# Cross-attention in float32 products: the values as seven block products, turned by way of DRAM and by block turns, and w_t x kept in DRAM

## The chip, the cores and the metric

The kernel runs on one core of one Trainium2 chip. The metric is the device time of one execution in microseconds; several runs are taken and the median is shown. A profile of one execution by the hardware profiler says which engine did what when. The engines are PE (matrix products; PEld are its weight loads), DVE (VectorE), ACT (ScalarE), POOL (GpSimd) and SP (SyncE, which here only issues transfers). Each works through a list of its own, in order, and waits on semaphores for the others.

## What is computed

The reference, cut to what matters, for B = 32 batches of x and y (`ctx_2048`) with C = 256 channels and N = 1024 places, all in float32:

```python
x_q = jnp.einsum('oc,bcn->bno', w_qk, y)
x_k = jnp.einsum('oc,bcn->bon', w_qk, x)
x_v = jnp.einsum('oc,bcn->bon', w_v, x) + b_v[None, :, None]
energy = jnp.einsum('bnc,bcm->bnm', x_q, x_k)
attention = jax.nn.softmax(energy, axis=-1)
attention = attention / (1e-07 + attention.sum(axis=1, keepdims=True))
x_r = jnp.einsum('bcn,bnm->bcm', x_v, attention)
x_r = jax.nn.relu(jnp.einsum('oc,bcn->bon', w_t, x - x_r) + b_t[None, :, None])
return x + x_r
```

## The kernel before

**The algebra.** The weights are multiplied with each other once at the start. Keys of a batch are k = -(w_qk^T w_qk) x, so that energy is -(y^T k). The values are multiplied by w_t beforehand: u = -(w_t w_v) x. What the output needs of x beside them is w_t x + b_t. So a batch needs k, u and w_t x from x, the energy from y and k, the softmax, and the sum of u over the attention.

**Exactness.** Every operand of a product is held as two float32r tiles, a high part (rounded, a copy on ACT) and a low part (what is left, a subtraction on POOL or DVE). A product is then three matmuls: high by high, high by low, low by high (`ORDER`).

**Seven products.** Keys, w_t x and energies are products of matrices cut in 2 x 2 blocks, done with seven block products instead of eight (the sums and differences of blocks that this takes are `x_sum`, `y_sum`, `key_sum` on the operands, and `key_block`, `x_block`, `energy_add`, `energy_block` on the results). A block product is 128 x 128 weights by 512 columns, so a batch takes 21 matmuls for k, 21 for w_t x and 4 x 21 for the energies. The values u are not done in this way before the change: they are needed with the place n on the partitions (as weights of the attention products), and `values` gets them so by taking pieces of x as weights and `vws` (w_t w_v, 256 columns) as what streams: 48 matmuls of 256 columns. ACT then takes the high parts from PSUM (`value_high`) and DVE the low parts (`value_low`), 128 x 1024 each, twice a batch.

**A batch.** Eight tiles of 128 rows of the energy, in four pairs `E0` to `E3` of seven products each. Each pair ends in blocks that DVE adds up while it takes the row's least (`energy_block`, a custom instruction and one that reads its accumulator). ACT takes the exponential, DVE the reciprocal of the sum, ACT the high part (`h`) and DVE the low part (`l`) of the shares, and DVE (for the first tile ACT) adds the shares up for the division by columns (`sum`, in `acc`). Products `A` (tile, half of channels c, half of columns h; three matmuls each, 96 a batch) add up u by the shares in PSUM banks 4 to 7. When all eight tiles are in, `cols`, `inv` and `turn` on DVE make the columns' inverse sums, `div` on DVE multiplies, `join` on POOL adds w_t x from the tile `xe`, `pos` on ACT is the relu, `add` is a transfer issued by POOL that adds x from DRAM, and `st` stores.

**PSUM.** Of eight banks, 0 to 3 hold energies and keys, 4 to 7 the attention; between `div` of one batch and the first `A` of the next, banks 4 to 7 serve the values and w_t x.

**The order** is written out by hand as three lists of words (`FIRST`, `STEADY` for each batch, `LAST`), where a + or - ahead of a word moves it one batch on or back. A word is a small function: `E0P1` is the first product of pair 0, `xP3` the third product of w_t x, `V01` half of the values. `InOrder` keeps the lists' order on PE, DVE, ACT and POOL; the transfers on SP have no such chain and stand as the scheduler puts them. Since `InOrder` issues everything, nearly every row of the profile bears its line, L62; instructions are told apart by the names of tiles: `gws`, `tws` the weights of k and w_t x, `xf` and `gf` the forms of x and k, `yd` and `ysum` those of y, `uf` those of u, `efs` those of the shares, `rs` results in passing, `raws` what is loaded, `z` the output.

Of the kernel before, what the change touches and what calls it, by code (L numbers as in the profile page):

```python
# [17 lines left out]
def kernel(  # L18
# [54 lines left out]
    def value(v):  # L73
        return v.bitcast(F32)

    class Ring:


        def __init__(self, name, places, shape, dtype=F32):
            self.tile = mem.tile([P, places, *shape], dtype, name=name)  # L80
            self.places, self.next, self.held = places, 0, {}

        def __getitem__(self, key):
            if key not in self.held:
                self.held[key] = self.tile[:, self.next % self.places]
                self.next += 1
            return self.held[key]
# [5 lines left out]
    RIGHT = {1: 0, 2: 2, 3: 3, 4: 7, 5: 4, 6: 6, 7: 5}  # L93
    T1, T3, T2, T4 = range(4, 8)
# [11 lines left out]
    vws = mem.tile([P, FORMS, KC, C], F32R, name="vws")  # L106
    xf = mem.tile([P, FORMS, 8, MB], F32R, name="xf")
# [6 lines left out]
    xe = mem.tile([P, KC, N], F32, name="xe")  # L114
    rct, rc = acc.rearrange("p (j r) -> p j r", r=G32), acc
    raws = Ring("raws", 2, [N])
    sums = Ring("sums", 4, [2, MB])
    efs = Ring("efs", 4, [FORMS, MH, MB], F32R)
    rs = Ring("rs", 4, [MB])
    small = Ring("small", 60, [1])  # L120
# [36 lines left out]

    gt, tt = (
# [4 lines left out]
    raws.held["y", 0, 0] = xe[:, 0]  # L163
# [4 lines left out]
    def load_y(b, q):  # L168
        load(
            raws["y", b, q].rearrange("p (k n) -> p k n", k=KC),  # L170
            y[b].rearrange("(k p) n -> p k n", p=P)[:, :, ts(q, MB)],
        )
# [71 lines left out]
    once("Sth", act.copy, tt[:, HIGH], wtT)  # L244
    once("Stl", pool.tensor_tensor, tt[:, LOW], wtT, value(tt[:, HIGH]), ALU.subtract)
# [40 lines left out]
    left_blocks("T", tws, lambda: wtT)  # L286

# [6 lines left out]

    def x_high(b, k):
        act.copy(flat(xf[:, HIGH, 2 * k : 2 * k + 2]), raws["x", b, k])

    def x_low(b, k):
        at = slice(2 * k, 2 * k + 2)
        pool.tensor_tensor(  # L300
            flat(xf[:, LOW, at]), raws["x", b, k], flat(value(xf[:, HIGH, at])), ALU.subtract
        )
# [19 lines left out]
    for k in range(KC):  # L322
        word(f"ldx{k}", load_x, k)
        word(f"ldy{k}", load_y, k)
        word(f"xh{k}", x_high, k)
        word(f"xl{k}", x_low, k)
        word(f"xTh{k}", sums_high, ("x13", "x24")[k], xf, slice(4 + 2 * k, 6 + 2 * k))
        word(f"xTl{k}", sums_low, ("x13", "x24")[k], xf, slice(4 + 2 * k, 6 + 2 * k))
# [6 lines left out]
    def products(name, bank, left, right, where, first):  # L335
        for i, w in zip((1, 2, 3, 4, 5, 6, 7), where):
            words[f"{name}P{i}"] = lambda b, i=i, w=w: product(
                banks[:, bank[w]], left(i), right(i), i in first
            )

# [4 lines left out]
        "k", KB, lambda i: lambda j: gws[:, j, LEFT[i]], lambda i: lambda m: xf[:, m, RIGHT[i]],  # L345
# [40 lines left out]
    for tail, name, at in ((0, "kA", KT3), (1, "kB", KT4)):  # L386
# [5 lines left out]
    XB = dict(a=6, b=4, c=5)  # L392
    products(
        "x", XB, lambda i: lambda j: tws[:, j, LEFT[i]], lambda i: lambda m: xf[:, m, RIGHT[i]],
        "abcacaa", (1, 2, 5),
    )
    xb = {w: banks[:, at] for w, at in XB.items()}

    def x_read(b, j):
        act.activation(rs["x", b, j], xb["a"], AF.Identity, bias=xbias[:, j // 3])  # L400

    def x_block(b, j, w, c, h):
        dve.tensor_tensor(xe[:, c, ts(h, MB)], xb[w], rs["x", b, j], ALU.add)

    for j in range(1, 4):
        word(f"xr{j}", x_read, j)
    word("xc11", x_block, 1, "b", 0, 0)
    word("xc22", x_block, 3, "c", 1, 1)
    word("xc12", x_block, 2, "c", 0, 1)
    word("xw21", lambda b: act.activation(xe[:, 1, :MB], xb["a"], AF.Identity, bias=xbias[:, 1]))  # L410

    VP = (2, 3)

# [475 lines left out]
```

## Time and profile before

| | |
|---|---|
| time, median of 3 runs (lowest to highest) | 1828.92 us (1828.8 to 1829.51) |
| span of the profiled execution | 1827.7 us, 1.2 us under the median |
| HBM read, written | 101.58 MB, 33.55 MB, 74 GB/s over the span |
| instructions | 25492, of them 8680 matmuls and as many weight loads |
| transfers | 66 loads of x and 64 of y on SP, 62 adding loads of x on POOL, 66 stores |
| PE in 40 equal slices of the span | 9 tenths or more in all, 8 in the last |

Busy times in the profile are unions of the instructions' times; a mean in a group is the length of one instruction, in which the start of the next can already lie. Idle time stands with what ended it.

### The profile page before, as it was taken

The numbers are of one execution on the slowest core, as the hardware profiler recorded it, in microseconds if no ns is written. First come the engines' busy times: TensorE is split into PE (matmuls) and PEld (weight loads), VectorE is DVE, ScalarE is ACT, GpSimd is POOL, SyncE is SP. The second block draws the span as 40 slices with busy tenths as digits, with TensorE's granted clock in tenths as the row PEclk, the third lists the DMA queues.
The fourth block names the chain that finished last, engine by engine and source line by source line (L and its number), as shares of the span: only waits on it lengthen the run. The fifth ranks groups of instructions, "written<-read, shape, count | busy, mean of one in ns | idle before, by whom it ended". The sixth has DMA issues, their size and how long they took to land. (4 is left out here: it accounts for less than half of the span.)

```text
span 1827.7 us, 25492 instructions
## 1 busy us (share of the span) xinstructions
PE 1819.0 (100%) x8680; PEld 1518.6 (83%) x8680; DVE 1683.3 (92%) x3200; ACT 1363.2 (75%) x2128; POOL 1365.8 (75%) x975
## 2 busy tenths in 40 slices
PE   9999999999999999999999999999999999999998
PEld 7888888888888888888888888888888888888886
DVE  6999999999999999999999999999999999999998
ACT  7778777777777787777877778777777777787765
POOL 7877777777787777877777777777777787777863
PEclk9999999999999999999999999999999999999999
DMA  2123232232312322223323223232332322323222
GB/s 90 47 81 89 61 81 58 81 93 58 92 52 76 93 62 89 66 62 92 78 74 81 58 81 92 59 82 58 81 93 58 93 51 77 93 62 89 58 81 69
DMA packets 46722, 136.78 MB, mean 75 GB/s; under 512 B 4480, under 2 KB 5376, under 8 KB 46592
## 3 DMA queue, kind: packets, MB, share of 16 engines
q1 hardware_dynamic: 37248, 102.25, 15.7%
q0 software_dynamic: 8928, 32.51, 10.8%
q8 instruction: 68, 1.11, 0.2%
q14 instruction: 62, 0.51, 0.1%
q10 hardware_dynamic: 416, 0.39, 0.1%
HBM read 101.58 MB, written 33.55 MB: 74 GB/s over the span
## 5 line engine op out<-in xcount | busy, mean ns | idle before, releaser
L62 PE MATMUL banks<-efs,uf 128*128 128x512 f32 x3072 | 763.5, 389 | 0.0
L62 PEld LDWEIGHTS banks<-efs,uf 128*128 128x128 f32 x3072 | 576.7, 188 | 120.4
L62 PE MATMUL banks<-gf,ysum 128*128 128x512 f32 x1524 | 411.1, 393 | 0.2
L62 ACT ACTIVATE banks<-banks,small 128x1024 f32<-128x1024 f32 x256 | 278.2, 1087 | 177.0 <-DVE small L62 174.5
L62 DVE SCALAR_TENSOR_TENSOR efs<-banks,small,efs 128x512 fp32r<-128x512 f32 x512 | 367.7, 744 | 4.2 <-ACT efs L62 1.4
L62 ACT ACTIVATE efs<-banks,small 128x512 fp32r<-128x512 f32 x512 | 339.8, 691 | 37.4 <-DVE small L62 15.2
L62 DVE SCALAR_TENSOR_TENSOR acc<-banks,small,acc 128x512 f32<-128x512 f32 x448 | 326.1, 746 | 10.6 <-ACT efs L62 5.6
L62 PEld LDWEIGHTS banks<-gf,ysum 128*128 128x128 f32 x1524 | 279.3, 188 | 66.7 <-POOL gf L62 11.2
L62 POOL TENSOR_TENSOR sums<-raws 128x256 f32<-128x256 f32 (+1 forms) x188 | 189.1, 1013 | 191.6 <-DMA raws<-in_ctx_dram 191.5
L62 PE MATMUL banks<-gf,yd 128*128 128x512 f32 x1158 | 307.3, 391 | 0.5 <-DVE rs L62 0.5
L62 PEld LDWEIGHTS banks<-gf,yd 128*128 128x128 f32 x1158 | 214.6, 188 | 46.2 <-DVE rs L62 1.8
L62 DVE CUSTOM_DVE_ANT_0 banks<-banks,rs,small 128x512 f32<-128x512 f32 x254 | 192.4, 758 | 34.8 <-PE banks L62 12.4
L62 ACT COPY rs<-banks 128x512 f32<-128x512 f32 (+1 forms) x286 | 167.2, 585 | 68.2 <-PE banks L62 67.8
L62 POOL TENSOR_TENSOR xf<-raws,xf 128x1024 fp32r<-128x1024 f32 x62 | 148.8, 2400 | 83.0 <-ACT xf L62 83.0
L62 PEld LDWEIGHTS banks<-vws,xf 128*128 128x128 f32 x1536 | 194.5, 191 | 10.1 <-DVE z L62 4.2
L62 PE MATMUL banks<-vws,xf 128*128 128x256 f32 x1536 | 198.7, 282 | 0.0
L62 POOL TENSOR_TENSOR gf<-sums,gf 128x1024 fp32r<-128x1024 f32 (+1 forms) x95 | 191.6, 2046 | 0.6 <-ACT gf L62 0.6
L62 DVE CUSTOM_DVE_ANT_0 banks<-banks,rs 128x512 f32<-128x512 f32 x254 | 179.8, 708 | 11.8 <-PE banks L62 0.5
L62 POOL TENSOR_TENSOR ysum<-sums,ysum 128x1024 fp32r<-128x1024 f32 x64 | 154.2, 2409 | 48.2 <-ACT ysum L62 48.2
L62 PE MATMUL banks<-xf,tws 128*128 128x512 f32 x651 | 177.3, 389 | 0.0
L62 PE MATMUL banks<-xf,gws 128*128 128x512 f32 x651 | 163.9, 391 | 0.0
L62 POOL TENSOR_TENSOR z<-z,xe 128x1024 f32<-128x1024 f32 x62 | 148.1, 2410 | 13.6 <-DVE z L62 13.6
(105 smaller groups left out, 2357.3 us busy)
## 6 DMA issues: line engine op xcount, KB each, us to landing
raws<-in_x_dram SPq DMA_DIRECT2D x66, 512.0 KB, 4.2
raws<-in_ctx_dram SPq DMA_DIRECT2D x63, 512.0 KB, 3.9
z<-in_x_dram POOLq DMA_DIRECT2D x62, 512.0 KB, 5.4
out_dram<-z SPq DMA_DIRECT2D x62, 512.0 KB, 3.1
out_dram<-z SPq DMA_DIRECT2D x4, 256.0 KB, 2.0
xe<-in_ctx_dram SPq DMA_DIRECT2D x1, 512.0 KB, 6.5
z<-in_L_xattn_w_t_dram ACTq DMA_DIRECT2D x1, 256.0 KB, 4.5
z<-in_L_xattn_w_v_dram SPq DMA_DIRECT2D x1, 256.0 KB, 5.6
```

The source lines that it names most:

```text
L62: self.last = getattr(self.engine, name)(*args, **kwargs)
```

## The change

**Values.** For batches 1 to 31, u is made as w_t x is: seven block products with weights `mws` (the blocks of w_t w_v and their sums), the right sides shared with those of k and w_t x (`products("u", ...)`). They come out with channels on the partitions. ACT reads bank a four times (`u_read`) and DVE adds three times (`u_block`); the four blocks of 128 x 512 lie in `rs` and are stored to a space in DRAM (`ud`). From there SP loads them in four transfers for each half of the tiles, so that 32 x 32 blocks come to lie where they belong (`u_loaded`, tile `turned`), DVE turns each block in place (`u_turned`), ACT takes the high parts (`u_high`) and POOL the low parts (`u_low`). All this is done a batch ahead. Batch 0 keeps `values`. The places of a half of the tiles are dealt out in blocks of 32, so y is loaded with the same deal, in pieces of 512 bytes, and `y_high` and `y_low` of its second half are two instructions each.

**w_t x** is also made a batch ahead. Its blocks lie in the same three places of `rs` as u's and are stored to another space in DRAM (`xd`); `xe` is gone, and `join` is a transfer issued by POOL that adds from there into `z`.

**Places.** Tiles that went round in turn (`Ring`) now have fixed places by name (`Places`). `xf` has seven forms instead of eight.

**All three lists are new.** Of these the diff shows one line each.

```diff
-    class Ring:
+    class Places:
...
-    vws = mem.tile([P, FORMS, KC, C], F32R, name="vws")
-    xf = mem.tile([P, FORMS, 8, MB], F32R, name="xf")
+    mws = mem.tile([P, FORMS, LEFTS, P], F32R, name="mws")
+    xf = mem.tile([P, FORMS, RIGHTS, MB], F32R, name="xf")
...
-    xe = mem.tile([P, KC, N], F32, name="xe")
+    turned = mem.tile([P, NB // NG, HT, G32], F32, name="turned")
...
-    rs = Ring("rs", 4, [MB])
+    rs = Places(
+        "rs",
+        {
+            ("e", 1): 0, ("e", 2): 1, ("e", 3): 2, ("k", 1): 0, ("k", 2): 1, ("k", 3): 2,
+            ("u", 1): 3, ("u", 2): 4, ("u", 3): 5, ("u", 4): 3,
+            ("x", 1): 3, ("x", 2): 4, ("x", 3): 5, ("x", 4): 3,
+            "F": 4, "corner": 0, "product": 1, "g": 5, "m": 3,
+        },
+        [MB],
+    )
...
+        for k in range(KC):
+            load(
+                y_raw(b, q).rearrange("p (k j n) -> p k j n", k=KC, j=NG)[:, k],
+                y[b].rearrange("(k p) (j h n) -> p k j h n", p=P, j=NG, h=MH)[:, k, :, q],
+            )
...
-    def x_block(b, j, w, c, h):
-        dve.tensor_tensor(xe[:, c, ts(h, MB)], xb[w], rs["x", b, j], ALU.add)
+    def x_block(b, j, w):
+        dve.tensor_tensor(rs["x", b, j], xb(b, w), rs["x", b, j], ALU.add)
+
+    def x_kept(b, j, c, h):
+        load(xspace[b % 2, ts(c, P), ts(h, MB)], rs["x", b, j])
...
+    products(
+        "u", ub, lambda i: lambda j: mws[:, j, LEFT[i]], lambda i: lambda m: xf[:, m, RIGHT[i]],
+        "abcacaa", (1, 2, 5),
+    )
+    def u_read(b, j):
+        act.copy(rs["u", b, j], ub(b, "a"))
+
+    def u_block(b, j, w):
+        dve.tensor_tensor(rs["u", b, j], ub(b, w), rs["u", b, j], ALU.add)
+
+    def u_kept(b, j, c, h):
+        load(uspace[b % 2, ts(c, P), ts(h, MB)], rs["u", b, j])
+
+    def u_loaded(b, h):
+        v = uspace[b % 2].rearrange("(a r) (j h t s) -> j r a h t s", r=G32, j=NG, h=MH, s=G32)
+        for j in range(NG):
+            load(turned[ts(j, G32)], v[j][:, :, h])
+
+    def u_turned(b, h):
+        v = turned.rearrange("p a t r -> p (a t r)")
+        dve.transpose(v, v)
...
+    def u_high(b, h):
+        act.copy(u_tiles(HIGH, h), u_from())
+
+    def u_low(b, h):
+        pool.tensor_tensor(u_tiles(LOW, h), u_from(), value(u_tiles(HIGH, h)), ALU.subtract)
...
     def joined(b, c):
-        pool.tensor_tensor(z[:, c], z[:, c], xe[:, c], ALU.add)
+        pool.dma_start(z[:, c], xspace[b % 2, ts(c, P)], accum_op=ALU.add)
...
     STEADY = """
-        E0P1 kTh0 -inv kTh1 kh22 E0r1 -turn kTl0 -A601 -A611 E0P6 yh11 E0P7 kTl1 E0r2 E0r3
+        E0P1 -A700 kTh1 ysh1 kTl1 +xT1 +xT2 E0r1 E0P7 E0P6 -cols E0r2 +xh1 uh0 +xTh0
```

Three places show how this moves the lists. The first is PE in a steady batch, among the energies of pairs E0 and E1 (`gf,ysum` and `gf,yd`). Before (`vws` are the values, `tws` w_t x):

```order
L62 MATMUL banks<-vws,xf 128x256 x12
L62 MATMUL banks<-gf,ysum 128x512 x3
L62 MATMUL banks<-vws,xf 128x256 x24
L62 MATMUL banks<-gf,yd 128x512 x3
L62 MATMUL banks<-vws,xf 128x256 x12
L62 MATMUL banks<-gf,ysum 128x512 x6
L62 MATMUL banks<-xf,tws 128x512 x3
```

and now:

```order
L62 MATMUL banks<-xf,mws 128x512 x6
L62 MATMUL banks<-xf,tws 128x512 x3
L62 MATMUL banks<-gf,yd 128x512 x3
L62 MATMUL banks<-xf,mws 128x512 x3
L62 MATMUL banks<-gf,ysum 128x512 x6
L62 MATMUL banks<-xf,mws 128x512 x6
L62 MATMUL banks<-gf,ysum 128x512 x3
L62 MATMUL banks<-xf,mws 128x512 x3
L62 MATMUL banks<-gf,yd 128x512 x3
L62 MATMUL banks<-xf,mws 128x512 x3
```

The 48 matmuls of the batch's own values are gone, and 21 of the next batch's (`mws`) stand among the energies instead.

The second place is DVE in the same steady batch, before at pair E1, where a low part of the values stands between two reductions of energies (ISA with `rs` is one, with `small` as a third input one that starts from the least of another):

```order
L62 TENSOR_TENSOR rs<-banks,rs 128x512
L62 ISA banks,small<-banks,rs 128x512
L62 ISA small 128x1
L62 TENSOR_TENSOR uf<-banks,uf 128x1024
L62 ISA banks,small<-banks,rs,small 128x512
L62 ISA small 128x1
L62 ISA banks,small<-banks,rs 128x512
L62 ISA small 128x1
L62 ISA banks,small<-banks,rs,small 128x512
L62 ISA small 128x1
```

and now at pair E2:

```order
L62 TENSOR_TENSOR rs<-banks,rs 128x512 x2
L62 ISA banks,small<-banks,rs 128x512
L62 ISA small 128x1
L62 ISA banks,small<-banks,rs 128x512
L62 ISA small 128x1
L62 ISA banks,small<-banks,rs,small 128x512
L62 ISA small 128x1
L62 TENSOR_TENSOR rs<-banks,rs 128x512
L62 ISA banks,small<-banks,rs,small 128x512
L62 ISA small 128x1
L62 RECIPROCAL small<-small 128x1
```

The low parts are gone from DVE, and adds of u and w_t x (`rs<-banks,rs`) and the turns of `turned` have come. E2's first reductions both stand ahead of the two that start from them, where E1's second pair before the change stood with nothing between.

The third place is SP in one steady batch. Before, a batch has six transfers there:

```order
L718 DMA out_dram<-z 128x1024
L166 DMA raws<-in_x_dram 128x1024
L169 DMA raws<-in_ctx_dram 128x2x512
L718 DMA out_dram<-z 128x1024
L169 DMA raws<-in_ctx_dram 128x2x512
L166 DMA raws<-in_x_dram 128x1024
```

and now:

```order
L210 DMA raws<-in_ctx_dram 128x4x128 x4
L486 DMA uspace<-rs 128x512
L491 DMA turned<-uspace 32x8x128 x4
L486 DMA uspace<-rs 128x512 x3
L459 DMA xspace<-rs 128x512 x4
L844 DMA out_dram<-z 128x1024
L200 DMA raws<-in_x_dram 128x1024
L844 DMA out_dram<-z 128x1024
L200 DMA raws<-in_x_dram 128x1024
L491 DMA turned<-uspace 32x8x128 x4
```

Twenty-four transfers stand where six stood: the loads of u's second half (`ul1`) stand between the first and the other three stores of the next batch's u, and those of the first half (`ul0`) at the end.

337 lines of the change are left out of this document (207 added, 130 removed).

## Prediction

> **What bounds the kernel now.** I read the page first, then the stages, then single instructions. The page gives each engine's busy time, its share of the span and its number of instructions:
>
> ```profile
> span 1827.7 us, 25492 instructions
> PE 1819.0 (100%) x8680; PEld 1518.6 (83%) x8680; DVE 1683.3 (92%) x3200; ACT 1363.2 (75%) x2128; POOL 1365.8 (75%) x975
> ```
>
> TensorE is never idle, but ends of matmuls are modelled, so a busy PE may still be a slow one. The timeline of PE inside one steady batch settles that (start, length and count of runs of like matmuls; two pieces of it):
>
> ```profile
> 868.63 1.59 PE L62 MATMUL banks<-vws,xf 128*128 128x256 f32 x12
> 870.05 0.86 PE L62 MATMUL banks<-gf,ysum 128*128 128x512 f32 x3
> 870.76 3.04 PE L62 MATMUL banks<-vws,xf 128*128 128x256 f32 x24
> ...
> 892.78 4.24 PE L62 MATMUL banks<-efs,uf 128*128 128x512 f32 x18
> 896.86 0.84 PE L62 MATMUL banks<-gf,yd 128*128 128x512 f32 x3
> ```
>
> The 18 matmuls of 512 columns from 892.78 give way to the next run at 896.86: 4.08 us, 0.2267 us apiece. The 24 of 256 columns start at 870.76 and take 3.04 us with the drain of the last (1.59 us for 12, so 12 more cost 1.45): 0.121 us apiece. Nothing stands between them, so PE is bound by its own stream, and a matmul that goes is time that goes. The only thing that PE waits for in the steady state is small:
>
> ```profile
> PEld banks L62 <- POOL gf L62: 11.2, 31, 0.5
> ```
>
> That is 0.36 us in each of 31 batches. The view by stages, with a window of about one batch, tells how far away the next bound is (busy time of PE, weight loads, DVE, ACT and POOL in turn), and the block turn that DVE does once a batch gives the period:
>
> ```profile
> 850.60:906.80 56.20, 56.20 (x270) 47.02 (x269) 52.25 (x101) 42.26 (x67) 42.59 (x31) 1.00 0.28 76
> ...
> 920.52 1.25 DVE L62 STREAM_TRANSPOSE acc<-sc 128x1024 f32<-128x1024 f32 x1
> ...
> 976.97 1.25 DVE L62 STREAM_TRANSPOSE acc<-sc 128x1024 f32<-128x1024 f32 x1
> ```
>
> The period is 976.97 - 920.52 = 56.45 us. At 52.25 in 56.20, DVE is busy for 52.5 us of it and has 4.0 us free. ACT and POOL have about 14 us free, the clock is granted in full, and DMA is busy for 0.28. So PE binds, with VectorE 4 us behind it.
>
> **PE.** Batches 1 to 31 lose the 48 value matmuls of 256 columns and get 21 of 512: 48 x 0.121 = 5.81 us against 21 x 0.2267 = 4.76 us. That is 1.05 us a batch; the total count of the rows before (1536 in a stream of which PE is never out) gives no better figure, so I take 1.0 us, and 31.0 us over 31 batches. PE's own period becomes 55.45 us. Batch 0 keeps the old form and gains nothing.
>
> **DVE.** These are the groups (count, then busy us and mean ns, then idle time before them):
>
> ```profile
> L62 DVE TENSOR_TENSOR rs<-banks,rs 128x512 f32<-128x512 f32 x189 | 130.2, 689 | 21.5 <-PE banks L62 16.8 <-ACT rs L62 0.8
> L62 DVE TENSOR_TENSOR uf<-banks,uf 128x1024 fp32r<-128x1024 f32 x64 | 78.2, 1222 | 0.1
> L62 DVE STREAM_TRANSPOSE acc<-sc 128x1024 f32<-128x1024 f32 x32 | 39.8, 1245 | 1.0
> L62 DVE SCALAR_TENSOR_TENSOR z<-banks,ubias,acc 128x1024 f32<-128x1024 f32 x62 | 79.2, 1278 | 0.0
> L62 DVE CAST xf<-raws 128x1024 fp32r<-128x1024 f32 x1 | 0.7, 695 | 4.4 <-DMA raws<-in_x_dram 4.4
> L62 DVE CUSTOM_DVE_ANT_0 banks<-banks,rs,small 128x512 f32<-128x512 f32 x254 | 192.4, 758 | 34.8 <-PE banks L62 12.4
> L62 DVE RECIPROCAL small<-small 128x1 f32<-128x1 f32 x256 | 40.7, 159 | 28.0 <-ACT banks L62 20.3
> ...
> 914.09 1.27 DVE L62 TENSOR_TENSOR banks<-banks,rs 128x512 f32<-128x512 f32 x2
> ...
> 912.93 1.24 DVE L62 TRANSPOSE_TENSOR_REDUCE parts<-acc 128x32 f32<-128x1024 f32 x1
> ```
>
> Means overlap the instruction behind by some 0.08 us: two adds that take 0.69 each are done in 1.27, so an add costs 0.60, and the 1.24 us at 912.93 gives way at 914.09, after 1.16. A batch loses two low parts of values (2 x 1.14 = 2.28), and gains three adds of u (3 x 0.60 = 1.80) and two block turns. No in-place turn of a tile loaded by DMA is in this trace; the nearest row is the turn of the same size and type, 1.245 us or 1.16 behind another, so 2.32 for two; bounds are 1.4 for the two (a cast of that size out of SBUF takes 0.695) and 2.6 (the slowest pass of 128x1024, `z`, takes 1.278). The lower one would make PE the bound (rival 1), the upper adds 0.3 us to the period. The adds of x keep their number and only write `rs` instead of `xe`. DVE's load becomes 52.5 - 2.3 + 1.8 + 2.3 = 54.3 us of 55.45: 1.15 us free instead of 4.0.
>
> How much of the 4.0 us must stay? Where the second reduction of an energy block takes the least of the first as its start, and stands right behind it, DVE stands for 0.15 us. This piece of its timeline shows it:
>
> ```profile
> 867.74 0.69 DVE L62 CUSTOM_DVE_ANT_0 banks<-banks,rs 128x512 f32<-128x512 f32 x1
> 868.34 0.14 DVE L62 DVE_READ_ACCUMULATOR2_ANT small<- 128x1 f32 x1
> 868.63 0.76 DVE L62 CUSTOM_DVE_ANT_0 banks<-banks,rs,small 128x512 f32<-128x512 f32 x1
> ```
>
> 868.34 + 0.14 = 868.48, and the next starts at 868.63. A batch has eight such pairs; in the old order six are neighbours, in the new one four (the change's rows on DVE show E2's, which are drawn apart): 0.6 us. Seven small steps of the inverse that wait for each other (0.03 each), eight reciprocals with some 0.04 behind each, and the chain of key sums (0.2) make 0.7 more. So about 1.3 us must stay where 1.15 is free: DVE would need 55.6 us for a batch and PE 55.45. The rest of today's idle time (16.8 us for PE at the group `rs`, 20.3 for ACT at the reciprocals, a little over 1 us a batch together) can only go if DVE never runs out of ready work; with two engines at their limit I leave 0.1 of it. **Period 55.7 us**, 0.75 less than now, 31 x 0.75 = 23.2 us.
>
> **A rule that speaks against this.** The Trainium skill (Perfetto Trace Analysis, Identifying the Most-Contended Engine) says that for Tensor the busy share of matmuls is no good measure, and that the share of weight loads is to be set against the occupancy of the others. By it the bound is DVE (92%) and not PE (83% for weight loads), and work moved from PE to DVE can only lose. The trace disagrees as far as PE goes: the runs above follow each other at 0.2267 us without a gap. What the rule would give is the slower rival below, 1886 us, so I keep a chance for it.
>
> **ACT, POOL, DMA: cover that is there.** Rows of what is added:
>
> ```profile
> L62 ACT COPY rs<-banks 128x512 f32<-128x512 f32 (+1 forms) x286 | 167.2, 585 | 68.2 <-PE banks L62 67.8
> L62 ACT ACTIVATE efs<-banks,small 128x512 fp32r<-128x512 f32 x512 | 339.8, 691 | 37.4 <-DVE small L62 15.2 <-PE banks L62 14.8 <-issue 0.2
> L62 ACT ACTIVATE banks<-banks,small 128x1024 f32<-128x1024 f32 x256 | 278.2, 1087 | 177.0 <-DVE small L62 174.5
> L62 ACT CAST uf<-banks 128x1024 fp32r<-128x1024 f32 x64 | 64.9, 1016 | 0.0
> L62 POOL TENSOR_TENSOR z<-z,xe 128x1024 f32<-128x1024 f32 x62 | 148.1, 2410 | 13.6 <-DVE z L62 13.6
> L62 POOL DMA_DIRECT2D z<-in_x_dram x62 | 53.4, 867 | 7.4 <-ACT z L62 7.4
> q1 hardware_dynamic: 37248, 102.25, 15.7%
> z<-in_x_dram POOLq DMA_DIRECT2D x62, 512.0 KB, 5.4
> out_dram<-z SPq DMA_DIRECT2D x62, 512.0 KB, 3.1
> out_dram<-z SPq DMA_DIRECT2D x4, 256.0 KB, 2.0
> ```
>
> ACT gets four copies of 0.585 (2.3 us) a batch, the high parts of values stay at about 1.0, and some 0.3 comes and goes with x and y: about 44.5 of 55.7. POOL gives up two adds of 2.41 (`join`) and takes two low parts of values of the same size; two more DMA issues of 0.87 are 1.7 us, and the shorter first half of x gives back 1.1: about 43.5. Both stay free for over 10 us, which covers this; without the cover it would be 2.3 and 0.6 us a batch. DMA gets 4 MB a batch on top of about 4.3 (four stores of u, eight loads of u, four stores of x, two adding loads of x): 0.28 becomes about 0.6, the pieces of 512 B included, still no bound. The round trip of u has room: `ul1` waits for POOL's `uL0`, which stands by E1's products, and `ut1` stands ahead of E3's first product, with some 63 matmuls of PE, 14 us, between E1's end and there; `ul0` has the 45 matmuls from E3's end to that of the key products, 10 us, less the 2.4 of POOL's `uL1`. Four loads that together take a store and a load of today (2.0 to 5.4 us each by the rows) fit. The adding `join` takes 5.4 us where POOL took 2.4, and only `pos`, `add` and `st` of a tile that is written 55 us later stand behind it.
>
> **Head and tail.**
>
> ```profile
> 1800.00:1815.00 15.00, 14.69 (x64) 11.46 (x63) 14.14 (x31) 8.92 (x14) 1.68 (x1) 1.00 0.34 103
> 1815.00:1828.00 13.00, 5.82 (x26) 4.50 (x24) 8.38 (x12) 0.00 (x0) 3.73 (x3) 0.81 0.22 81
> ```
>
> At the end DVE sets the pace (14.14 of 15.00 busy), so matmuls taken out of the last batch may not shorten it: between 0 and 5 us of the gain is lost there, and I take 2. The head does more for batch 1 earlier; what moves there is gone later, and I take 0 (between -2 and +4).
>
> **The sum.** 1827.7 - 23.2 + 2 = 1806.5 us of span. The median of the runs shown, 1828.92, is 1.2 above the span: **1807.7 us**, put as 1808.
>
> **Rivals.**
>
> 1. PE's own pace. The order hides all that DVE must wait for, and the period is 55.45: 1827.7 - 31.0 + 2 + 1.2 = 1800 us (1795 without the loss at the end and with some of PE's 0.36 us waits gone). For it: PE is fully fed today. Against: 54.3 + 1.3 is over 55.45. Chance 0.2.
> 2. The stores hold ACT. u and x share three places of `rs`, so `xr1` can write only when the store of `ur4` (`ud4`) has landed. Between the two ACT has an exponential and a high part, 1.1 + 0.7 us, against 2.0 us to land a 256 KB store, plus its wait in SP's queue behind `ul1`. Behind `xr1` stand high parts and exponentials, for which DVE waits. A wait of 0.5 to 0.8 us that passes to a DVE without slack gives periods of 56.2 to 56.5: 1823 to 1833 us, near no change. ACT's 11 us of free time speak against it. Chance 0.15.
> 3. Slower: DVE becomes the bound with its waits of today. If it goes on standing for 4.0 us a batch, whoever it waits for, the period is 54.3 + 4.0 = 58.3: 1827.7 + 31 x 1.85 + 1.2 = 1886 us. It decides from 2.15 us of idle time a batch on (56.45 - 54.3); I see 1.3 that must stay, and today's rows show about 1 us that ended with PE or ACT. Chance 0.15.
>
> That the change does not remove the matmuls can be left out: the rows of PE's order show 21 where 48 stood.
>
> **Chances.** The forecast (periods 55.55 to 56.1, 1803 to 1820 us) has 0.5. With rival 1 and the better half of rival 2, faster by over 0.2% (under 1825.3, about what a measurement of this kernel can tell from no change) has 0.75; within 0.2% has 0.10; slower 0.15. The range of 1795 to 1832 us takes in the first rival and most of the second and leaves the third out.
>
> **What would show it.** The rows `xf,mws` should come 0.2267 us apart and the period should be 55.5 to 56 us. DVE should be busy for 54 to 54.6 us of it, the two turns at 1.2 to 1.3 us each, and its idle time should be mostly the 0.15 us stops. PE should show its first real waits, for DVE (weight loads held by `banks<-DVE`), some 0.3 us a batch. Wrong would be: turns far from 1.25 us, DVE idle for over 2 us a batch, `turned` or `rs` waited for by DMA for more than a fraction of a microsecond, or a tail longer by over 5 us.

## The result, and the profile after

| | before | after |
|---|---|---|
| time, median of 4 runs (lowest to highest) | 1829.17 us (1828.8 to 1829.51) | 2164.05 us (2161.0 to 2166.32) |
| ratio to before, 95% interval | | 1.183 (1.1814 to 1.1847) |
| span of the profiled execution | 1827.7 us | 2159.0 us |

The change costs 335 us; 1808 was forecast, so the prediction was wrong in sign and far outside its range. The page of after, the line of busy times:

```profile
PE 1937.6 (90%) x7843; PEld 1473.9 (68%) x7843; DVE 1743.4 (81%) x3295; ACT 1440.1 (67%) x2322; POOL 1399.5 (65%) x1108
```

837 matmuls are gone, as they should be, and nobody is busy all the time any more. One period, from one block turn of `acc` to the next (start, length), and the view by stages for just that stretch (length, busy time and count of PE, weight loads, DVE, ACT and POOL, clock, DMA share, GB/s):

```profile
1041.92 1.23 DVE L62 STREAM_TRANSPOSE acc<-sc 128x1024 f32<-128x1024 f32 x1
...
1109.12 1.23 DVE L62 STREAM_TRANSPOSE acc<-sc 128x1024 f32<-128x1024 f32 x1
```

```profile
1041.92:1109.12 67.20, 60.34 (x245) 45.95 (x244) 54.44 (x105) 44.94 (x73) 43.66 (x35) 0.95 0.46 126
```

This batch takes 67.20 us instead of 56.45. The work itself came out as forecast: 245 matmuls at 0.2267 are 55.5 us, and DVE is busy for 54.4. The engines stand and wait.

Where the loss lies, the same view says for longer stretches: from the first exponential of batch 0 to that of batch 1, and from there to that of batch 31. Before:

```profile
24.79:79.42 54.63, 54.41 (x236) 42.74 (x235) 48.52 (x93) 41.07 (x65) 50.41 (x42) 1.00 0.12 39
79.42:1772.59 1693.17, 1692.96 (x8096) 1415.80 (x8095) 1575.32 (x3002) 1273.21 (x1980) 1281.66 (x901) 1.00 0.27 75
```

After:

```profile
25.18:105.48 80.30, 69.69 (x289) 52.85 (x288) 53.58 (x100) 51.32 (x85) 60.33 (x59) 0.96 0.27 85
105.48:2104.87 1999.39, 1801.34 (x7278) 1370.74 (x7277) 1631.95 (x3090) 1341.81 (x2153) 1306.47 (x1017) 0.96 0.47 126
```

Of the 331.3 us between the two spans, 306.2 lie in the 30 batches of the long stretch (66.65 us each instead of 56.44), and 25.7 in the one stretch ahead of them, the head.

For whom the engines wait, says the view of waits (us in total, times, longest):

```profile
PEld banks L62 <- ACT rs L62: 235.2, 158, 6.3
...
PE banks L62 <- ACT rs L62: 170.6, 65, 5.9
DVE efs L62 <- ACT efs L62: 158.8, 120, 4.6
...
ACT rs L62 <- DMA uspace<-rs: 116.7, 31, 4.7
ACT efs L62 <- DVE acc L62: 92.9, 93, 2.0
```

PE waits for ACT to empty a bank into `rs`, ACT waits once a batch for a store of u, and DVE and ACT wait for each other. SP's queue has waits of its own, those of the loads of u (L491) among them:

```profile
SPq L491 <- POOL uf L62: 236.8, 60, 6.1
```

The timelines of SP, POOL, ACT and PE in one period show how PE's wait comes about; I put the rows in the order of the chain:

```profile
1051.56 0.35 SPq L486 DMA_DIRECT2D uspace<-rs  x1
1058.11 1.88 SPq L491 DMA_DIRECT2D turned<-uspace  x4
1060.09 2.45 SPq L486 DMA_DIRECT2D uspace<-rs  x3
```

```profile
1055.69 2.39 POOL L62 TENSOR_TENSOR uf<-turned,uf 128x1024 fp32r<-128x1024 f32 x1
```

```profile
1066.54 0.69 ACT L62 ACTIVATE rs<-banks,xbias 128x512 f32<-128x512 f32 x1 [3.94 <-DMA uspace<-rs]
```

```profile
1060.65 1.52 PE L62 MATMUL banks<-xf,tws 128*128 128x512 f32 x6
1067.28 1.65 PE L62 MATMUL banks<-xf,tws 128*128 128x512 f32 x3 [5.11 <-ACT rs L62]
1068.72 1.48 PE L62 MATMUL banks<-efs,uf 128*128 128x512 f32 x3
1070.00 1.48 PE L62 MATMUL banks<-gf,yd 128*128 128x512 f32 x3
1071.28 1.23 PE L62 MATMUL banks<-gf,ysum 128*128 128x512 f32 x3
1072.34 0.86 PE L62 MATMUL banks<-xf,tws 128*128 128x512 f32 x3
```

`ul1` may overwrite `turned` only when POOL's `uL0` has read it, at 1055.69 + 2.39 = 1058.08. It stands in SP's queue ahead of the other three stores of u, which so leave at 1060.09 and later, behind four loads. They land slowly, too (median us from issue to landing, view of DMA issues):

```profile
uspace<-rs SPq DMA_DIRECT2D x124, 256.0 KB, 5.5
```

`xr1` writes the place of `rs` that one of them reads, so ACT stands for 3.94 us, and PE, with no bank to write into, starts 5.3 us late (six matmuls from 1060.65 end their turn at 1062.01). That is not all: the next nine need 1071.28 - 1067.28 = 4.00 us instead of 2.04, and three more 1.06 instead of 0.68. The stages show why (clock is the number behind POOL's):

```profile
1060.00:1064.00 4.00, 2.17 (x10) 1.47 (x8) 3.15 (x8) 0.85 (x3) 2.66 (x3) 1.00 0.76 148
1064.00:1070.00 6.00, 2.73 (x7) 2.15 (x7) 1.54 (x4) 3.40 (x6) 0.00 (x0) 0.60 0.55 177
1070.00:1080.00 10.00, 10.00 (x41) 8.04 (x40) 7.53 (x16) 7.65 (x13) 2.77 (x5) 0.90 0.34 91
```

While PE stands, the granted clock falls: 0.60 is the mean of the stage, and narrower windows of the same view show 1.00 up to 1065 and 0.50 from 1065.5 to 1072. The three matmuls from 1068.72 come 0.427 us apart instead of 0.2267. So the late store takes 5.3 + 2.3 = 7.6 us of PE in this period.

### The profile page after: what moved, and what is told of

Same layout as the page of the kernel before. It is cut to its first block, busy times and chain, and to the rows that moved or that the text cites. A ratio compares the mean times of both kernels' runs of the same rounds, so it can differ in the third digit from the quotient of the medians.

```text
span 2159.0 us, 25689 instructions
## 1 busy us (share of the span) xinstructions
PE 1937.6 (90%) x7843; PEld 1473.9 (68%) x7843; DVE 1743.4 (81%) x3295; ACT 1440.1 (67%) x2322; POOL 1399.5 (65%) x1108
## 4 chain that ended last, share of the span: by engine, by line
PE 57%; DVE 13%; ACT 11%; DMA 9%; POOL 5%; issue 4%; SPq 1%; ACTq 0%; DVEq 0%; POOLq 0%
PE banks L62 57%; DMA uspace<-rs 8%; ACT efs L62 5%; DVE acc L62 4%; DVE efs L62 3%; ACT banks L62 3%; DVE banks L62 2%; ACT rs L62 2%; POOL sums L62 2%; POOL xf L62 1%; POOL gf L62 1%; DVE rs L62 1%; ACT acc L62 1%; SPq L491 1%; POOL uf L62 1%
## 5 line engine op out<-in xcount | busy, mean ns | idle before, releaser
L62 PE MATMUL banks<-gf,ysum 128*128 128x512 f32 x1524 | 443.9, 411 | 33.5 <-ACT rs L62 18.8
L62 ACT ACTIVATE efs<-banks,small 128x512 fp32r<-128x512 f32 x512 | 338.8, 689 | 123.7 <-DVE acc L62 92.9
L62 PE MATMUL banks<-gf,yd 128*128 128x512 f32 x1158 | 339.6, 411 | 18.4 <-DVE rs L62 8.8
L62 PE MATMUL banks<-xf,tws 128*128 128x512 f32 x651 | 205.0, 435 | 150.4 <-ACT rs L62 150.4
L62 POOL DMA_DIRECT2D z<-in_x_dram x62 | 63.2, 1024 | 421.5 <-ACT z L62 421.5
L62 ACT COPY rs<-banks 128x512 f32<-128x512 f32 (+1 forms) x410 | 237.6, 588 | 115.6 <-PE banks L62 111.0
L62 DVE TENSOR_TENSOR rs<-banks,rs 128x512 f32<-128x512 f32 x375 | 254.4, 685 | 37.9 <-ACT rs L62 28.7
L62 POOL TENSOR_TENSOR yd<-raws,yd 128x256 fp32r<-128x256 f32 x189 | 161.5, 923 | 186.1 <-ACT yd L62 183.3
L62 PEld LDWEIGHTS banks<-xf,tws 128*128 128x128 f32 x651 | 134.0, 212 | 191.8 <-ACT rs L62 164.4
L62 PE MATMUL banks<-xf,mws 128*128 128x512 f32 x651 | 185.7, 401 | 8.3 <-ACT efs L62 0.7
L62 ACT ACTIVATE rs<-banks,xbias 128x512 f32<-128x512 f32 x125 | 86.2, 689 | 142.5 <-DMA uspace<-rs 112.3
```

Of the source, the lines that this page charges most:

```text
L62: self.last = getattr(self.engine, name)(*args, **kwargs)
```

## The experiments

All are timed in three rounds beside the kernel before (1829 us). "New lists" are `FIRST`, `STEADY` and `LAST` of the change.

### SP's order: e1 and e2

The first theory is that chain. e1 lets SP keep the order of the lists, as the other engines do; in them `ul1` stands behind all stores of u:

```diff
-    pe, dve, act, pool = (InOrder(g) for g in (nc.tensor, nc.vector, nc.scalar, nc.gpsimd))
-    load = nc.sync.dma_start
+    pe, dve, act, pool, sp = (
+        InOrder(g) for g in (nc.tensor, nc.vector, nc.scalar, nc.gpsimd, nc.sync)
+    )
+    load = sp.dma_start
```

> The changed kernel with one edit: SP's transfers are chained in the order of the lists too, as PE, DVE, ACT and POOL are. Theory A (SP's order): in the changed kernel the four loads of u's second half stand ahead of three of the stores of u and wait for POOL's low part, so the stores leave late, ACT waits for them before it overwrites their places in rs (116.7 us in all), PE stands for 5 us a batch and then runs at 0.427 us a matmul for a while. With the stores ahead of the loads, ACT's wait for uspace falls below 40 us, the period from 67 us to 55.5 to 60, the time to 1805 to 1950 us. Theory B (the transfers themselves: 8.3 MB a batch where there were 4.3): stores go on landing after 5 us or more, ACT's wait stays over 90 us, time over 2080 us. Theory C (VectorE at 98%): DVE is busy for over 97% of the period and the time is about 1886 us.

e2 changes one thing in SP's queue, the four loads go behind the last four stores of u:

```diff
+    behind = []
+
     def u_kept(b, j, c, h):
-        load(uspace[b % 2, ts(c, P), ts(h, MB)], rs["u", b, j])
+        behind.append(load(uspace[b % 2, ts(c, P), ts(h, MB)], rs["u", b, j]))
...
-            load(turned[ts(j, G32)], v[j][:, :, h])
+            with ExitStack() as behind_all:
+                for d in behind[-4:]:
+                    behind_all.enter_context(tc.issue_after(d.ins))
+                load(turned[ts(j, G32)], v[j][:, :, h])
```

> The changed kernel with one edit: the loads of u wait in SP's list for the four stores of u traced last; nothing else of SP's list moves (stores of u four in a row, then the four loads). Theory A: this one swap is the cause, so most of what the order by lists gives comes here too: ACT's wait for uspace below 40 us, time below 1980 us and within 3% of the order by lists. Theory A' (SP's list as a whole is bad, not this swap): the order by lists gains and this does not, time over 2080 us. Theory B: neither gains, both over 2080 us. Theory C: about 1886 us with DVE busy for over 97% of the period.

e1 took 2027.38 us (ratio 1.108, 1.1063 to 1.1096), e2 2031.76 (1.1106, 1.1088 to 1.1125). Both gained less than was expected, but the swap alone is worth 132 us, the whole order of SP 137. The amount of the transfers is the same as in after, so it was not their amount that made the stores slow: in e2 the stores of u land in 2.1 us instead of 5.5. In e1 ACT's wait is gone and the one between ACT and DVE has grown (92.9 us in after):

```profile
ACT efs L62 <- DVE acc L62: 118.9, 122, 2.0
...
ACT rs L62 <- DMA uspace<-rs: 3.8, 3, 2.7
```

137 us are 4.4 a batch, not 7.6: waits that the stop had covered take the place of the rest. 198 us stay.

### Two engines on one bank: e4, e3, e6

The timelines of ACT and of DVE in e1 show the next pattern (`efs` of ACT are high parts, `acc` of DVE sums, `efs` of DVE low parts):

```profile
1056.09 0.69 ACT L62 ACTIVATE efs<-banks,small 128x512 fp32r<-128x512 f32 x1 [1.74 <-DVE acc L62]
1058.25 0.69 ACT L62 ACTIVATE efs<-banks,small 128x512 fp32r<-128x512 f32 x1 [0.90 <-DVE acc L62]
```

```profile
1055.24 0.75 DVE L62 SCALAR_TENSOR_TENSOR acc<-banks,small,acc 128x512 f32<-128x512 f32 x1
1056.81 0.75 DVE L62 SCALAR_TENSOR_TENSOR efs<-banks,small,efs 128x512 fp32r<-128x512 f32 x1 [0.81 <-ACT efs L62]
1057.47 0.74 DVE L62 SCALAR_TENSOR_TENSOR acc<-banks,small,acc 128x512 f32<-128x512 f32 x1
1058.97 0.75 DVE L62 SCALAR_TENSOR_TENSOR efs<-banks,small,efs 128x512 fp32r<-128x512 f32 x1 [0.76 <-ACT efs L62]
```

DVE adds up a half of a tile, ACT waits and takes its high part, DVE waits and takes the low part. The low part reads the high part (`efs` is among its inputs), so it waits for ACT in any order. But neither the sum nor the high part reads what the other writes: both only read the bank, yet take turns, in the order of the lists. The old lists mostly give DVE the sum of one half (`sum30 l31`) while ACT takes the other; in the new ones tile 3 has `sum31 h31 l31`, all on one half, and tiles 5 and 7 have a sum and a high part of one half beside each other. The Trainium skill (PSUM — Partial Sum Buffer, PSUM bank collisions raise a hardware error) says that reads of ACT and DVE of one bank must not meet and that the compiler orders such pairs; these rows show that order. e4 puts this pattern into the kernel before, by swapping the halves of the sums of tiles 3, 4, 6 and 7 and nothing else:

```diff
-        ri3 xP5 xr2 +ldx1 h31 exp2 xc11 sum30 l31 xP7 sum31 A100 A000 xr3 ri2 h30 xc22
+        ri3 xP5 xr2 +ldx1 h31 exp2 xc11 sum31 l31 xP7 sum30 A100 A000 xr3 ri2 h30 xc22
...
-        sum41 +xl1 A210 A200 sum50 l50 h41 E3r1 l41 +yh01 l40 E3P6 sum40 -st1 +ldy1 E3P7
+        sum40 +xl1 A210 A200 sum50 l50 h41 E3r1 l41 +yh01 l40 E3P6 sum41 -st1 +ldy1 E3P7
...
```

> The kernel before, with one edit to STEADY: for tiles 3, 4, 6 and 7 the words sum..0 and sum..1 change places, so that ACT's high part and DVE's sum stand side by side on the same half of a tile. Theory D: each of the four pairs makes one engine wait for the other for some 0.6 us; DVE has 4 us a batch free and hides part of it: 1840 to 1900 us, with ACT's wait for DVE acc (below 1 us in all before) over 40 us. Against theory D: 1829 us within 0.3%.

It took 1957.77 us (1.0701, 1.0685 to 1.0717): 128 us from the order of four tiles' sums alone, more than was expected. Three waits of e4:

```profile
ACT efs L62 <- DVE acc L62: 63.9, 68, 1.5
DVE acc L62 <- ACT efs L62: 59.6, 116, 1.1
...
PE banks L62 <- DVE acc L62: 29.3, 29, 1.0
```

Before has no row of the first and the third kind, and of the second

```profile
DVE acc L62 <- ACT efs L62: 5.6, 29, 0.2
```

The third is of another kind than the first two: the moved sum of tile 4 (`sum41`) now reads the bank that `E3P7` writes, and PE stands for it once a batch. So the 128 us are not all turns of ACT and DVE, and no run takes the two apart.

The reverse was tried on e1: e3 swaps the halves for tiles 0, 1, 2, 3, 5 and 7. For tiles 1 and 2 a sum then reads a bank that the next product has overwritten, so their sums are not the reference's.

```diff
...
-        E1P3 +uc2 +ur4 exp3 +ud4 +ud2 +ud3 E1c11 ri3 A111 +xP2 E1c12 sum31 h31 +xr1 l31
-        sum30 +xP5 h30 exp2 +xP6 A011 +xr2 l30 E2P1 ri2 h21 +xc1 sum21 E2P7 +xP7 E2r1
+        E1P3 +uc2 +ur4 exp3 +ud4 +ud2 +ud3 E1c11 ri3 A111 +xP2 E1c12 sum30 h31 +xr1 l31
+        sum31 +xP5 h30 exp2 +xP6 A011 +xr2 l30 E2P1 ri2 h21 +xc1 sum20 E2P7 +xP7 E2r1
...
```

> The order-by-lists kernel (2027 us, period 62.35 us) with one edit to STEADY: for tiles 0, 1, 2, 3, 5 and 7 the words sum..0 and sum..1 change places, so that while ACT takes the high part of one half of a tile, DVE adds the shares of the other half, as the lists before the change mostly had it. Theory D (two engines on one bank take turns): in the new lists ACT's high part and DVE's sum stand side by side on the same half, and one waits for the other each time (ACT efs for DVE acc 118.9 us, DVE efs for ACT efs 74.6, DVE acc for ACT efs 44.9). With the halves apart ACT's wait for DVE acc falls below 50 us and the time to 1870 to 1970 us. Theory R (what is left comes from the transfers of u, x and y and the places in rs): within 1% of 2027 us. Theory V (VectorE's load): DVE's idle time just moves to other waits, time within 1% of 2027 us, and leaving out work on DVE helps more.

2024.53 us (1.1068, 1.1051 to 1.1084), within 3 us of e1 and not the 1870 to 1970 expected: ACT's wait for `acc` fell to 51.8 us, but the moved sums of tiles 1 and 2 now wait for the product ahead of them:

```profile
DVE acc L62 <- PE banks L62: 41.7, 29, 1.4
ACT acc L62 <- PE banks L62: 37.0, 29, 1.3
```

e6 swaps only where nothing moves behind a product, tiles 3, 5 and 7.

> The order-by-lists kernel (2027 us) with sum..0 and sum..1 exchanged in STEADY for tiles 3, 5 and 7 alone, where no energy product overwrites the half that is added later. e3 had moved those of tiles 1 and 2 behind products that overwrite their bank, and they waited for PE in turn. Theory D (ACT and DVE take turns on a bank): ACT's wait for DVE acc falls from 118.9 us to below 60, the stop of PE ahead of the second product of w_t x (33.3 us in 1400) goes, time 1950 to 1995 us. Theory R (transfers and places): 2027 us within 0.5%.

1981.35 us (1.0827, 1.0811 to 1.0844): 46 us less than e1. The wait falls to a quarter, and the store's wait, which the turns had covered, is back:

```profile
ACT rs L62 <- DMA uspace<-rs: 37.9, 31, 3.1
...
ACT efs L62 <- DVE acc L62: 29.8, 62, 2.0
```

### VectorE's load and the way through DRAM: e5 and e8

Two rivals. e5 is e3 without the block turns (the values are left unturned), 2.3 us less of DVE in each batch:

> The kernel of e3_lists_halves_apart without DVE's two block turns of u a batch (leaves out the turning of u's 32 x 32 blocks). Takes 2.3 us a batch, 71 us in all, off DVE. Theory V: the time falls by 45 to 75 us against e3_lists_halves_apart. Theories D and R (engines wait for each other in the order of the lists): by less than 25 us.

2003.56 us (1.095, 1.0931 to 1.0968), 21 us less than e3. e8 is e1 without `ud`, `ul`, `ut`, `uh` and `uL`: u is computed and goes nowhere, the attention uses what lies in `uf`.

> The order-by-lists kernel without u's way after its products (leaves out the stores and loads of u, the block turns and the high and low parts of u; later batches use batch 0's values; u's products, reads and adds stay, and so do the lists). Takes 2 MB of transfers, 2.3 us of DVE, 2.1 of ACT and 4.8 of POOL a batch away. Theory R: 1800 to 1880 us. Theory D and the order of the lists: over 1950 us.

1998.76 us (1.0922, 1.0903 to 1.094), 29 us less than e1, and still 169 us slower than before. In e8 the turns and the way of u are both gone, and most of the loss stays. But e5 and e8 stand on e3 and e1, where other waits can cover what such an edit gains (e14 below shows a case), and the way of w_t x through DRAM stays in both. What the turns and the ways through DRAM are worth in the best form, e12, was not run.

### Single waits: e7, e9 to e12, e14

e7 is put on e6, e9 on e7, e10 and e11 each on e9, e12 on e11. e7 moves `sum10`, for which exp0 waited, behind `E1r1`; e9 gives blocks 1, 3 and 4 of w_t x the places 5, 3, 5 of `rs` and stores u's third block right behind its sum; e10 puts tile 1's low part ahead of `div0` and both its sums ahead of `E0c12`.

```diff
-        +xTl0 sum11 l11 E0c12 l10 E1P1 +ur1 +uc1 +uP6 sum10 exp0 xd2 +ldy0 +ud1 ri0 E1r1
+        +xTl0 sum11 l11 E0c12 l10 E1P1 +ur1 +uc1 +uP6 exp0 xd2 +ldy0 +ud1 ri0 E1r1 sum10
```

> e6_halves_apart_three with the word sum10 (on ACT for tile 1) moved behind E0's second exponential and E1's first read, just ahead of the product that overwrites its bank. In the order-by-lists kernel ACT stands for 1.7 us a batch there for DVE's low part of the same half, and the reads of E1 and u behind it hold PE (0.56 and 0.78 us a batch). Theory D: ACT's wait of acc for DVE efs (49.4 us) falls below 15 us and the time by another 25 to 50 us. Theory R: no change within 0.5%.

> The kernel of the run before (1977.6 us), with w_t x's blocks 1, 3 and 4 in other places of rs (5, 3, 5 instead of 3, 5, 3) and the store of u's third block issued right behind its sum, so that xr1 waits for a store issued about 4 us earlier. What is left there: ACT waits 41 us in all for uspace<-rs, and PE stops ahead of tws. Theory that what is left is single waits in the order: ACT's wait for uspace<-rs falls from 41 us to under 8, the stop of PE ahead of tws goes, and with it 0.6 to 1.3 us a batch, so 1937 to 1960 us. Rival, that the waits stand in series and whatever is taken out comes back at the next one: the wait falls just as much, but the time stays within 8 us of 1977.6, and another wait on banks or acc grows by about as much.

> The kernel of the run before this one (e9), with tile 1's words in another order: the low part of its second half ahead of div0 and of the sums, and both of ACT's sums of this tile ahead of DVE's reduction E0c12, so that DVE's low part and ACT's sum work on different halves. Theory of single waits: E1P7 no longer waits for sum10 (about 1.4 to 1.8 us on PE in each batch so far, PEld and PE on ACT acc 53 and 40 us in all), and 0.7 to 1.5 us a batch go: 20 to 47 us under e9. Rival, waits in series: PE's wait on ACT acc goes and PE's wait on DVE efs (l10, now behind E0c12) or on DVE rs takes its place, within 10 us of e9 or slower.

Three misses: 1977.64 us, 1981.22 and 1979.39, all within 4 us of e6. In e7 PE waits at `E1P7` for the sum that ACT no longer waits behind; in e10 that wait becomes one for `div0`, which reads `acc`. In e9 the wait for the store stayed (44.3 us), now at the second block, `xr2`. Its view of DMA issues gave the reason: over the windows of 1028 to 1031 us and 1031 to 1033 us,

```profile
uspace<-rs SPq DMA_DIRECT2D x2, 256.0 KB, 2.0
...
uspace<-rs SPq DMA_DIRECT2D x1, 256.0 KB, 5.0
```

The late one is issued at 1032.0; POOL's timeline has `join1`, the adding transfer of w_t x, right ahead of it:

```profile
1030.83 0.85 POOL L62 DMA_DIRECT2D z<-xspace  x1
1031.44 2.69 POOL L62 TENSOR_TENSOR ysum<-sums,ysum 128x1024 fp32r<-128x1024 f32 x1
```

e11 puts `join1` behind that instruction of POOL:

```diff
-        E1P7 +ur2 -join0 +ys01 +ys02 +ys04 uL0 -join1 sum01 sum00 h01 l01 E1P6 +yh00
+        E1P7 +ur2 -join0 +ys01 +ys02 +ys04 uL0 sum01 sum00 h01 l01 E1P6 +yh00
...
-        sum31 +xP5 h30 exp2 +xP6 A011 +xr2 l30 E2P1 ri2 h21 +xc1 sum21 E2P7 +xP7 E2r1
+        sum31 +xP5 h30 exp2 +xP6 A011 +xr2 -join1 l30 E2P1 ri2 h21 +xc1 sum21 E2P7 +xP7 E2r1
```

> The kernel of e9 (1981.2 us) with join1, the second adding transfer z<-xspace, issued by POOL one instruction later (behind the low part of y's sums, 1033.8 instead of 1030.8 in the period looked at). In e9 the store of u2 that was issued at 1032.0, beside that transfer, took 5.0 us to land, the other three 2.0, and ACT's xr2 waited 0.94 us for it. If transfers that lie beside each other are what makes the store late: it lands in 2.0 to 2.6 us, ACT's wait for uspace<-rs falls from 44 us to under 10, PE's stop ahead of tws (22 us in 1100, about 1.2 us a batch with the slow matmul behind it) goes, and the time falls by 15 to 38 us, to 1943 to 1966. If waits stand in series: ACT's wait falls just as much, and the time stays within 8 us of 1981. If the store's 5 us has another cause: the wait stays at 35 to 45 us.

1939.67 us (1.06, 1.0582 to 1.0617), 41.6 less than e9, a little more than expected. The wait is gone (4.5 us in all instead of 44.3).

e12 then puts `E1P6` ahead of `E1P7`, so that PE has a product that does not need tile 1's bank:

> The kernel of e11 with E1's sixth product ahead of its seventh, as pair E3 has them, so that PE has 0.68 us of work that needs no bank of tile 1 while ACT adds up sum10. Single waits: PE's stop for ACT acc (93 us, 3 us a batch by both kinds) falls by about 0.68 us a batch, 15 to 25 us under e11. Waits in series: PE stops at E1P6 for E1r1 instead (rs), and the time stays within 8 us of e11.

1931.39 us (1.0548, 1.0518 to 1.0577), 8 us less than e11: about half of the least that was expected of a single wait (15 us), since PE now stops for `E1r1` (its timeline shows 0.79 us at that place). With e13 below it is the fastest form with the change, and slower than the kernel before.

e14 puts the edits of e9 and e11 on e1, without those of e6 and e7:

> The kernel of e1 (2027.4 us, SP's queue in the lists' order) with e9's places and store and e11's later join1, and no change in the order of tile 1's, 3's, 5's or 7's words. Between e7 and e11 these were worth 38 us. If transfers and turns on a bank add up: 1980 to 1995 us. If the turns cover the transfers' wait (DVE and ACT stand for each other anyway): 2010 to 2025. If the wait for the store costs more there, since it holds up turns too: under 1975.

2027.29 us (1.109, 1.1071 to 1.1108), nothing gained on e1's 2027.38. So the two costs do not add up: as long as ACT and DVE wait for each other on a bank, they cover the late store, and what the transfers cost shows only when the turns are gone.

### The rest: e13, e15, e16

e13 is e12 with two waits between DVE and ACT taken out, at tiles 1 and 4:

```diff
-        +xTl0 sum11 l11 E0c12 l10 E1P1 +ur1 +uc1 +uP6 exp0 xd2 +ldy0 +ud1 ri0 E1r1 sum10
+        +xTl0 l11 sum11 E0c12 l10 E1P1 +ur1 +uc1 +uP6 exp0 xd2 +ldy0 +ud1 ri0 E1r1 sum10
...
-        exp4 sum51 h50 l51 A001 ri4 ut1 E3P1 l50 sum41 A200 h40 E3r1 h41 E3P6 E3P7 l41
-        E3r2 l40 A300 E3P5 E3r3 E3P4 sum40 uh1 E3c22 E3P2 E3c21 +yh10 +yh11 E3P3 E3c11
+        exp4 sum51 h50 l51 A001 ri4 ut1 E3P1 l50 h40 sum40 A200 E3r1 h41 E3P6 E3P7 l41
+        sum41 E3r2 A300 E3P5 E3r3 l40 E3P4 uh1 E3c22 E3P2 E3c21 +yh10 +yh11 E3P3 E3c11
```

> The kernel of e12 (1931.4 us) with two more swaps in the list: tile 1's low part ahead of its sum (DVE stands 0.76 us there for ACT, ACT then 1.07 us for DVE, PE 0.95 us ahead of E1P6), and tile 4's halves dealt so that DVE adds up one half while ACT takes the high part of the other (DVE stands 0.76 us for ACT, ACT 0.67 us for DVE, PE 0.45 us ahead of the product behind E3r3). If what is left over the kernel before (102 us, 3.3 us a batch, as much as PE stands still) is made of such single waits: 0.8 to 1.4 us a batch go, 1888 to 1907 us. If the waits stand in series: within 8 us of 1931, other stops of PE grow by as much.

1931.24 us (1.0568, 1.0548 to 1.0587), no gain. PE now waits for the keys' low parts, which POOL makes (22 us by both rows in e12):

```profile
PEld banks L62 <- POOL gf L62: 48.0, 31, 2.6
PE banks L62 <- POOL gf L62: 35.2, 27, 2.2
```

Part of it may be the clock: its mean over the profiled execution is 0.991 in e13 and 0.998 in e12. By the difference of these means, 0.007 of 1937 us, an estimate of what it took is 14 us at most.

e15 moves two of POOL's instructions for x of the batch after next (`xT3`, `xl0`) behind those low parts, and e16 also issues the load `ldy1`, for which POOL stood 275 us in e13, with `ldy0`:

> The kernel of e13 (1931.2 us) with two of POOL's instructions, x's sum xT3 and x's low part xl0 for the batch after next (1.3 us each), moved behind the keys' low parts. In e13 the two waits of DVE and ACT are gone, but PE waits 83 us for POOL's gf instead of 23 (1.02 us ahead of E0's second product in the period looked at). If these are single waits whose gain in e13 was taken by POOL: PE's wait for gf falls under 20 us, and 25 to 45 us go, 1886 to 1906. If POOL is held by its loads and only stands elsewhere: within 8 us of 1931.

> The kernel of e15 with the load of y's second half (ldy1) issued right behind that of the first, so that it no longer stands in SP's queue behind ul1 and xd1. In e13 POOL stood for that load 9.1 us in each batch (275 us in all), and the keys' low parts behind it came late. If that late load is what makes POOL late: POOL's wait for in_ctx falls under 60 us, and the time is 10 to 30 us under e15. If POOL only waits elsewhere (for ACT's yd, or PE): within 8 us of e15. If the loads now lie beside the stores of u and w_t x: ACT's wait for uspace comes back, and the time is over that of e15.

1953.45 us (1.0679, 1.0661 to 1.0697) and 1956.84 (1.0691, 1.0675 to 1.0707): both slower than e13 by over 20 us, which no forecast for e15 had. In e15 PE waits for x's forms instead, which u and w_t x need a batch ahead, and 41.9 us for `div` on DVE, for which it stood 0.5 us in e13. In e16 POOL's wait for `ldy1` is gone from its waits, and another has come, in the adding transfer of x:

```profile
POOL z L62 <- ACT z L62: 181.7, 30, 6.8
PEld banks L62 <- ACT xf L62: 49.9, 28, 1.9
```

## Why the prediction was wrong

| what was undone, one on the other | us | less |
|---|---|---|
| after | 2164.05 | |
| SP's order (e1) | 2027.38 | 136.7 |
| sums of three tiles on the other half (e6) | 1981.35 | 46.0 |
| a store beside an adding transfer (e7, e9, e11) | 1939.67 | 41.7 |
| E1's sixth product first (e12) | 1931.39 | 8.3 |
| left over before | | 102 |

The shares hold for this order of undoing only, as e14 shows. By the spans of the profiles e12 is 100.1 us over before: 74.0 in the 30 batches from the first exponential of batch 1 on (58.91 us each), 23.7 ahead of it, 2.4 behind them.

**PE's term was right.** 21 matmuls of u take the place of 48; where PE is fed, they come 0.23 us apart (in after six from 1054.08 give way at 1055.46).

**DVE's load was right.** 54.4 us were found, 54.3 forecast, and the turns take the length of their nearest row:

```profile
L62 DVE STREAM_TRANSPOSE turned<-turned 128x1024 f32<-128x1024 f32 x62 | 76.4, 1232 | 0.0
```

**The step that failed first is "The round trip of u has room".** It counted PE's matmuls between the place of `ul1` in the lists and that of its user, and asked whether the loads come in time. They do: DVE's waits in after have no row for `turned`. What was not asked there is who stands behind them: `ul1` waits for POOL at the head of SP's queue, and the three stores behind it are what ACT waits for. The rows of SP's order were there, with `ul1` between the first store and the rest. e2 shows that this place alone costs 132 us.

**Rival 2 had the mechanism and less than a fifth of the price.** It named `xr1`, `ud4` and SP's queue behind `ul1`, and put 0.5 to 0.8 us on them. The wait was 3.94 us on ACT, 5.3 on PE, and 2.3 more by the low clock; the net price by e1 is 4.4 us a batch. Its stores were priced at the 2.0 us of an undisturbed one, and landed in 5.5. "ACT's 11 us of free time speak against it" was wrong: free time elsewhere in the batch does not shorten a wait at a place where PE needs the bank.

**"About 1.3 us must stay" failed too.** It counted stops inside DVE's own stream and took the rest of the idle time as free to go. In the new lists DVE and ACT stop each other, up to four times a tile; the old ones mostly avoid this. e6 shows it, with 46 us taken out of the new kernel, and so does e4, with up to 128 put into the one before (PE's waits for a moved sum among them). DVE idle for over 2 us a batch and `rs` waited for by DMA were two of the prediction's own signs of being wrong, and both came. The lists that the order was read from have both words beside each other (`sum31 h31`); the sum treated ACT and DVE as loads, not as a pair on one bank.

**The head was put at 0, "between -2 and +4", and cost 25.7 us.** The reason given was that what moves there is gone later. The 42 matmuls for u and w_t x of batch 1 are 9.5 us of it, and about that much does come back: the last of the 30 stretches takes 57.8 us, some 9 less than the others. The rest is stops and a slower clock: PE is busy for 69.69 of the 80.30 us there, where it was for 54.41 of 54.63. In e12 the same stretch still takes 22.0 us more than before. No run has an edit of `FIRST`, where this order stands, so what it could be is open.

**Rival 3 had the right sign and not the cause.** 1886 us were to come from DVE as the bound with its old waits. But DVE is idle for 67.2 - 54.4 = 12.8 us a batch in after, not 4.0, and e5, which takes 2.3 us of its load away, gains 0.7 a batch.

**What stays open.** In e12 102 us are left, about 2.5 a batch and some 24 ahead of the batches. In the batches they stand as stops of PE for ACT, DVE and POOL at several places, and three more edits (e13, e15, e16) moved them or added to them. Whether some order of the seven-product form has as few stops as the old order, or whether making x's forms, u and w_t x a batch ahead always puts too much beside the keys, is not settled.

## What to carry to other kernels

When a load is added to a queue, ask what it waits for and price that wait for everything queued behind it, down to the engine that sets the pace. A sum of busy times says what a schedule could reach, not what it will: where two engines read the same PSUM bank, count their turns in the order given. Judge a mended wait only when those that cover it are gone, since the edits of e9 and e11 were worth nothing on e1 and 38 us on e7. And where work is moved a batch ahead, price the batch that has none ahead of it: the head took 26 us here.

## What the hardware showed unasked

In after the granted clock fell to 0.50 a little over 3 us into a stop of 5.3 us and stayed there until about 1072, so matmuls came 0.427 us apart for some 4.8 us after the stop. The Trainium skill (TensorE: Matmul & The Clock Gate, Part 1: The HAM clock gate) describes this: half clock after an idle window of about 3.4 us, 426.7 ns for 512 columns. The trace agrees, and the stop of 0.79 us in e12 leaves the rate as it was. Behind that one only the first matmul is slower (starts of 1054.62, 1054.95, 1055.19 and 1055.42), and six take 1.49 us instead of 1.36:

```profile
1054.62 1.66 PE L62 MATMUL banks<-gf,ysum 128*128 128x512 f32 x6 [0.79 <-ACT rs L62]
1056.11 1.53 PE L62 MATMUL banks<-xf,mws 128*128 128x512 f32 x6
```

And a store of 256 KB issued 1.2 us behind an adding transfer of 512 KB took 5.0 us to land where its neighbours took 2.0. By the stages of e9 around them, 1028.0 to 1030.8 us and from there to 1037.0, the DMA engines' share is 0.76 and 0.81, which hardly tells the two apart: a mean share does not say how long a transfer takes. By what the adding transfer delays the store was not tried.
